# The last half row's queries in two parts, with ScalarE taking all weights in every second step

## The chip, the cores and the metric

The kernel runs on one core of a Trainium2 chip. Its engines work side by side, each through its own list of instructions in order: PE (TensorE: matrix products, with a separate row PEld for its weight loads), DVE (VectorE), ACT (ScalarE), POOL (GpSimd) and SP (SyncE, which here only issues DMAs). The metric is device time in microseconds. An effect on a few operations near the end of one stage is measured against a run of over 1.6 ms, so the numbers below are kept to tenths and hundredths of a microsecond.

## The reference, cut to what matters

The model has two attention and two feed-forward layers on x of shape (4, 1024, 256), all in float32. The change touches the second attention layer and the hand-over to the last layer, a mixture of experts:

```python
def _L1_attn_ref(x, w_qkv, w_out, b_out, gamma, beta):   # 16 heads of 16
    q, k, v = ...                                        # from x @ w_qkv
    scores = einsum('bhqd,bhkd->bhqk', q, k) / sqrt(16)
    w = relu(scores)
    attn = w / (sum(w, axis=-1, keepdims=True) + 1e-6)
    out = einsum('bhqk,bhkd->bhqd', attn, v) ... @ w_out + b_out
    return layernorm(x + out) * gamma + beta

x = x + layernorm(L1_attn(layernorm(x)))
x = x + layernorm(L1_ffn(layernorm(x)))                  # experts

# in L1_ffn, for all 4096 tokens together:
S = sigmoid(xt @ Wg).T          # 8 experts x 4096 tokens
G, I = top_k(S, 1024)           # each expert picks its tokens
```

So every token must have passed the whole attention layer, its layer norms and the gating product before any expert can choose its tokens: the top-k needs all logits.

## The kernel before

**Stages.** The first attention and feed-forward layer fill the span up to about 418 us, the second attention layer (the pool `st3` in the code) runs to about 1096 us, then come a search for each expert's threshold, the gathers, and the experts. Tokens are worked in blocks of 512 (`TB`), two to a sequence (`BPB = 2`); the text calls a block a half row, `t` = 0 to 7. A block has four tiles of 128 tokens (`NJ = 4`).

**A step of the attention.** For each half row the loops run over four groups of heads (`NG = 4`, four heads each) and eight tiles of keys (`KT = 8`): 32 steps. `scores` (L1233) writes four 32-row products of 512 queries into four PSUM banks at once; two of the banks (`sc1`) go through relu on ScalarE (L1242, 128x512 each), the other two (`sc2`, one 128x1024 tile) on VectorE (L1243). `weigh` (L1249) multiplies the weights with the values, four products into the four 32-row bands of the accumulator `po`. Program order on PE is scores of step n+1, then weighing of step n. The profile counts two instructions for each float32 product, so a step's four products appear as x8. The three banks with the tag "s" serve both the single scores (two a step) and, through `side`, all other products of the stage.

**After a group** `finish` turns `po` back (L1281); after every second group `divide` puts two pieces in front of the list `rest`: `by_weight` (L1110 to L1112, the division by the sum) and `back` (L1120, which writes `oT`). After the last group `close` adds the output projection `project_out` (L1135, added to the residual at L1142), and for each of the four tiles: `stats_y` (L1064 to L1067: statistics on VectorE, the power -1/2 on POOL), `affine` (L1155, L1156), a second statistics piece, `shift` (L1160 on VectorE, L1162 on ScalarE), `add` (L1167), `stats_x`, and `token_rows` (L1178, with DMAs to `tok_d` and `x_d`). Then come `turn_gating` (PE transposes, L1193, a ScalarE copy, L1196) and `gate` (L1207, added into `logits` at L1215).

**What sets the order.** PE, VectorE and ScalarE run in the order in which the code is written out (`manual_schedule`). Pieces wait in two lists, `beside` (with PE work) and `rest`. `go_on(room)` takes one piece of `beside`, if there is one, and `room` pieces of `rest`, double after a piece of `beside`; the main loop calls it once a step, with room 1, or 0 in a group's last step. So a half row's closing pieces run beside the steps of the next half row. The last half row has no next one: its pieces run after the last step, with `keep_busy` (L206, idle products of 512 columns in bfloat16) on PE, 8 and 63 of them. DMA issues on SP are placed by the framework.

**Afterwards** the gating stage begins with `keep_busy(idle, 9)` and 15 rounds of a threshold search on VectorE, with one small PE product each.

Of the kernel before, what the change touches and what calls it, by code (L numbers as in the profile page):

```python
# [18 lines left out]
P = 128  # L19
D = 256  # L20
# [51 lines left out]
def kernel(  # L72
# [968 lines left out]
    with ExitStack() as st3:  # L1041
# [25 lines left out]
            nc.gpsimd.tensor_tensor(rs, ve, mhalf[:, 0:1], ALU.pow)  # L1067
            return mv[:, 0:1], rs

        def by_tile(*steps):  # L1070

            kept = {}

            def run(do, i):
                kept[i] = do(i, *kept.get(i, ())) or ()

            return [lambda do=do, i=i: run(do, i) for do in steps for i in range(NJ)]

        def normalize(row, b, k):

# [21 lines left out]

        def divide(state, t):

            got, oT, closing = state["turned"], state["oT"], state.get("close")
            even = wk.tile([P, TB // 32, 2, HD], F32, tag="even", name="even", bufs=1)

            def by_weight():
                den = small.tile([P, 2, TB // 32], F32, tag="den", name="den")
                nc.vector.tensor_scalar(den, got[:, :, :, HD], KEPS, None, ALU.add)  # L1110
                nc.vector.reciprocal(den, den)
                nc.vector.tensor_tensor(  # L1112
                    even.rearrange("p b r d -> p r b d"),
                    got[:, :, :, 0:HD],
                    den.unsqueeze(3).to_broadcast([P, 2, TB // 32, HD]),
                    ALU.mult,
                )

            def back():
                nc.vector.transpose(oT[:, t, :], even.rearrange("p b r d -> p (b r d)"))  # L1120
                if t:
                    beside.extend(closing)

            return [by_weight, back]

        def close(t, h, oT):

            y = wk.tile([P, NJ, D], F32, tag="y", name="y")

            def project_out(z):  # L1130
                pt = side([P, 2, D], "pt")
                for k in range(2):
                    i = 2 * z + k
                    for c in range(DC):
                        nc.tensor.matmul(  # L1135
                            pt[:, k, :],
                            lhsT=oT[:, c, i * P : (i + 1) * P],
                            rhs=wop[:, c, :],
                            start=(c == 0),
                            stop=(c == DC - 1),  # L1140
                        )
                nc.vector.tensor_tensor(y[:, 2 * z : 2 * z + 2, :], pt, h[:, 2 * z : 2 * z + 2, :], ALU.add)  # L1142
                for k in range(2):
                    after(2 * z + k)

            def after(i):
                rest.append(after_out.pop(0))
                if i == NJ - 1:
                    rest.extend(after_out)

            def stats_y(i):
# [20 lines left out]
            def token_rows(i, mean, rs):  # L1172
                if t < ADDED:
                    nc.sync.dma_start(out_flat[t][:, i, :], xs[t][:, i, :])
                if i == 0:
                    gating["h"] = wk.tile([P, NJ, D], F32, tag="hg", name="hg")
                hg = gating["h"][:, i, :]
                nc.vector.tensor_scalar(hg, xs[t][:, i, :], mean, rs, ALU.subtract, ALU.mult)  # L1178
                nc.sync.dma_start(tok_d[t * TB + i * P : t * TB + (i + 1) * P, 0:D], hg)
                if i == NJ - 1:  # L1180
                    nc.sync.dma_start(x_d[t * TB : (t + 1) * TB, :].rearrange("(j p) d -> p j d", p=P), xs[t])
                if i % 2:
                    beside.append(lambda: turn_gating(i - 1))
                if i == NJ - 1:
                    beside.append(gate)

            def turn_gating(i0):
                if i0 == 0:
                    gating["hT"] = wk.tile([P, DC, TB], F32, tag="hT", name="hTg")
                tp = side([P, DC, 2, P], "tpg")  # L1190
                for c in range(DC):
                    for i in range(2):
                        nc.tensor.transpose(  # L1193
                            tp[:, c, i, :], gating["h"][:, i0 + i, c * P : (c + 1) * P], ident
                        )
                nc.scalar.copy(  # L1196
                    gating["hT"][:, :, i0 * P : (i0 + 2) * P], tp.rearrange("p c i t -> p c (i t)")
                )

            def gate():  # L1200

                b, half = divmod(t, BPB)
                pg = side([P, SEG], "pg")
                for c in range(DC):
                    for u in range(TB // SEG):
                        z = half * (TB // SEG) + u
                        nc.tensor.matmul(  # L1207
                            pg[32 * z : 32 * (z + 1), :],
# [2 lines left out]
                            start=(c == 0),  # L1211
                            stop=(c == DC - 1),
                        )
                rows = slice(64 * half, 64 * (half + 1))
                nc.vector.tensor_tensor(logits[rows, :], logits[rows, :], pg[rows, :], ALU.add)  # L1215

            gating = {}
            after_out = by_tile(
                stats_y, affine, lambda i: scale_of("c", y[:, i, :]), shift, add, stats_x, token_rows
            )  # L1220

            for z in range(2):
                yield lambda z=z: project_out(z)

        def scores(row, qh, g, kt):

            t, r = divmod(g, 2)
            w = wts.tile([P, 4, TB], F32, tag="w", name="w")
            singles = [ps.tile([P, TB], F32, tag="s", name="sc1", bufs=3) for _ in range(2)]
            pair = ps.tile([P, 2, TB], F32, tag="d", name="sc2", bufs=2)  # L1230
            for j, sc in enumerate((*singles, pair[:, 0, :], pair[:, 1, :])):
                rows = slice(32 * j, 32 * (j + 1))
                nc.tensor.matmul(  # L1233
                    sc,
                    lhsT=row["kT"][t][rows, r, kt * P : (kt + 1) * P],
                    rhs=row["qT"][rows, t, qh * TB : (qh + 1) * TB],
                    start=True,
                    stop=True,
                )

            for j, sc in enumerate(singles):
                nc.scalar.activation(w[:, j, :], sc, AF.Relu)  # L1242
            nc.vector.tensor_scalar(w[:, 2:4, :], pair, 0.0, None, ALU.max)  # L1243
            return w

        def weigh(row, g, kt, w):
            t, r = divmod(g, 2)
            for j in range(4):
                nc.tensor.matmul(  # L1249
                    po[32 * j : 32 * j + HD + 1, :],  # L1250
                    lhsT=row["v"][:, kt, HQ * t + 2 * j + r, :],
                    rhs=w[:, j, :],
                    start=(kt == 0),
                    stop=(kt == KT - 1),
                )

# [3 lines left out]
        def go_on(room=1):  # L1262
# [3 lines left out]
            for _ in range(room):  # L1266
                if rest:
                    rest.pop(0)()

        state = {}  # L1270

        def finish(row, b, qh, g, kt, w):
            t, r = divmod(g, 2)
            if g == 0 and kt == 0:
                state["oT"] = wk.tile([P, DC, TB], F32, tag="oT", name="oT")
            weigh(row, g, kt, w)
            if kt == KT - 1:

                if r == 0:
                    state["turned"] = wk.tile([P, 2, TB // 32, 32], F32, tag="turned", name="turned")  # L1280
                nc.vector.transpose(state["turned"][:, r].rearrange("p b d -> p (b d)"), po)  # L1281
                if g == NG - 1:
                    state["close"] = [
                        *close(b * BPB + qh, row["h"][qh], state["oT"])
                    ]
                if r:
                    rest[:0] = divide(state, t)

        row = row0
# [3 lines left out]
        for b in range(B):  # L1293
            after = open_row() if b + 1 < B else None
            for qh in range(BPB):
# [2 lines left out]
                    nc.scalar.activation(spare, row["h"][qh][:, 0, 0:1], AF.Exp)  # L1298
                if after is not None:
                    *steps, last = normalize(after, b + 1, qh)  # L1300
                    rest.extend((*steps, lambda last=last, to=(after, qh): (last(), beside.extend(project(*to)))))
                for g in range(NG):
                    for kt in range(KT):
                        w = scores(row, qh, g, kt)
                        if before is not None:
                            finish(*before)

                        go_on(0 if kt == KT - 1 else 1)
                        before = (row, b, qh, g, kt, w)
            row = after  # L1310
        finish(*before)
        idle = ps.tile([P, 2, TB], F32, tag="d", name="idle", bufs=2)[:, 0, :]
        keep_busy(idle, 8)
        while rest and not beside:
            go_on()
        while beside:
            go_on()

        keep_busy(idle, 63)
        while beside or rest:  # L1320
            go_on()
    both.close()


# [2 lines left out]
    with ExitStack() as st4:  # L1327
# [27 lines left out]
        with ExitStack() as sa:  # L1355
# [7 lines left out]
            nc.vector.tensor_scalar(sc, sc, 1.0, None, ALU.add)  # L1363
            nc.vector.reciprocal(sc, sc)
            idle = ps.tile([P, TB], F32, tag="idle", name="idle", bufs=1)
            keep_busy(idle, 9)

            def by_token(src, name):
                pt = ps.tile([P, SEG // P, NSEG * NE], F32, tag="tp", name=name)
# [450 lines left out]
```

## Time and profile before

| what | us |
|---|---|
| median of 3 runs (1630.39 to 1633.67) | 1633.25 |
| the profiled execution | 1633.18 |
| its span, first to last instruction | 1631.2 |
| last half row, first scores (L1233) start | 993.82 |
| its last weighing (L1249) ends | 1069.48 |
| last addition into the logits (L1215) ends | 1096.26 |

Times inside the run are counted from the start of the span. In the lists of instructions each line gives start, length, engine, line of the code, operation, what is written and read with its shape, the count where several like instructions are merged, and in brackets how long the engine had been idle before and what ended that. In the chain of work that ended last, each piece is followed back to what released it; lines give start, length, engine and what was done. Groups give the total busy time and the mean in ns of one.

### The profile page before, as it was taken

To read this page: it belongs to the slowest core of one execution; us is meant where nothing else is said; L and a number is where in the kernel's file an instruction comes from. 1 tells how busy PE (TensorE), PEld (TensorE's weight loads), DVE (VectorE), ACT (ScalarE), POOL (GpSimd) and SP (SyncE) were. 2 spreads that over 40 slices of the span, in tenths; PEclk is the share of its full clock that TensorE was granted. 3 is DMA by queue.
4 is the path that set the end of the run, shared out by engine and by line. 5 is a ranking of instruction groups with operands and counts; after the bars stand their busy time and mean duration, and the time that the engine had idled before them with its cause. 6 is when DMAs were issued, how large, how long until landed. Compare 5 with 4: busy or idle time off the path is not lost.

```text
span 1631.2 us, 22623 instructions
## 1 busy us (share of the span) xinstructions
PE 1569.7 (96%) x8787; PEld 778.2 (48%) x8787; DVE 920.7 (56%) x2085; ACT 634.7 (39%) x1101; POOL 403.3 (25%) x439
## 2 busy tenths in 40 slices
PE   7999999999999999999999999983999999999997
PEld 3666666666322232222323222231757667566674
DVE  4555566664657787878787888878211211222145
ACT  3344444544544545454545454521121121211233
POOL 4123232222201011111111001010423324324555
PEclk9999999999999999999999999995999999999999
DMA  8300000000000000101010100040133233234355
GB/s 205 120 1 1 1 1 1 0 1 1 1 1 1 23 18 7 34 7 34 1 40 1 39 2 27 14 168 4 53 78 69 66 74 72 66 75 89 65 148 136
DMA packets 70069, 71.15 MB, mean 44 GB/s; under 512 B 23597, under 2 KB 62922, under 8 KB 69834
## 3 DMA queue, kind: packets, MB, share of 16 engines
q1 hardware_dynamic: 56080, 47.01, 9.4%
q0 software_dynamic: 13008, 21.77, 7.4%
q8 instruction: 69, 1.13, 0.3%
q10 hardware_dynamic: 874, 0.93, 0.2%
q14 instruction: 38, 0.31, 0.1%
HBM read 41.74 MB, written 27.95 MB: 43 GB/s over the span
## 4 chain that ended last, share of the span: by engine, by line
PE 92%; DVE 4%; issue 1%; POOL 1%; ACT 1%; DMA 1%; POOLq 0%; SPq 0%; DVEq 0%; ACTq 0%
PE sc L1233 16%; PE po L1249 16%; PE ph L1712 13%; PE py L1735 13%; PE pg L691 4%; PE py L799 4%; PE pv L707 3%; PE ph L855 2%; PE po L771 2%; PE pt L1135 2%; PE pv L380 2%; PE pq L356 2%; PE pq L876 2%; PE po L775 2%; PE pk L356 2%; PE pkv L786 1%
## 5 line engine op out<-in xcount | busy, mean ns | idle before, releaser
L1243 DVE TENSOR_SCALAR w<-sc 128x1024 f32<-128x1024 f32 x256 | 312.7, 1222 | 97.4 <-PE sc L1233 65.1
L1242 ACT ACTIVATE w<-sc 128x512 f32<-128x512 f32 x512 | 278.0, 594 | 229.6 <-PE sc L1233 102.5
L1233 PE MATMUL sc<-qT,kT 32*128 32x512 f32 x2048 | 293.6, 639 | 1.4 <-ACT w L1242 0.8
L1249 PE MATMUL po<-w,vaug 128*17 128x512 f32 x2048 | 274.7, 598 | 1.3 <-DVE turned L1281 0.3
L1735 PE MATMUL py<-w,hid 128*128 128x256 f32 x1024 | 230.1, 380 | 0.0
L1719 ACT ACTIVATE hid<-ph,mb 128x512 f32<-128x512 f32 (+1 forms) x136 | 90.1, 662 | 344.4 <-PE ph L1712 343.3
L1712 PE MATMUL ph<-xT,w 128*128 128x512 f32 (+1 forms) x544 | 222.8, 567 | 0.7 <-DVE xT L1696 0.7
L1735 PEld LDWEIGHTS py<-w,hid 128*128 128x128 f32 x1024 | 191.1, 190 | 32.0 <-issue 7.0
L1233 PEld LDWEIGHTS sc<-qT,kT 32*128 32x128 f32 x2048 | 80.7, 183 | 184.9 <-issue 170.7
L1712 PEld LDWEIGHTS ph<-xT,w 128*128 128x128 f32 x544 | 103.2, 190 | 111.1 <-issue 107.6
L1249 PEld LDWEIGHTS po<-w,vaug 128*17 128x17 f32 x2048 | 35.3, 95 | 200.3 <-issue 171.0
L1754 POOL DMA_INDIRECT acc_d<-y,idx x56 | 88.1, 1573 | 157.0 <-issue 131.8
L1752 DVE TENSOR_TENSOR y<-py,mb 128x256 f32<-128x256 f32 x56 | 23.4, 418 | 142.3 <-PE py L1735 140.3
L1521 POOL DMA_INDIRECT got<-tok_d,idx x64 | 65.8, 1028 | 152.1 <-DVE idx L1511 135.0
L1696 DVE COPY xT<-tp 128x512 f32<-128x512 f32 (+1 forms) x34 | 22.3, 660 | 91.7 <-PE tp L1691 91.7
L1067 POOL TENSOR_TENSOR rsg<-veg,mhalf 128x1 f32<-128x1 f32 x32 | 17.7, 554 | 219.5 <-DVE veg L1066 219.5
L691 PE MATMUL pg<-nT,wh 128*128 128x512 f32 x128 | 61.4, 611 | 1.5 <-ACT nT L630 1.5
L799 PE MATMUL py<-wo,oT 128*128 128x256 f32 x256 | 61.9, 385 | 0.0
L707 PE MATMUL pv<-wh,nT 128*128 128x512 f32 x128 | 59.7, 592 | 0.0
L1511 DVE CAST idx<-parts 128x8 int32<-128x8 f32 x8 | 1.3, 167 | 101.8 <-PE parts L1509 101.8
L799 PEld LDWEIGHTS py<-wo,oT 128*128 128x128 f32 x256 | 47.3, 190 | 17.2 <-issue 9.4
L572 POOL TENSOR_TENSOR x<-x,y 128x1024 f32<-128x1024 f32 x14 | 32.9, 2351 | 73.3 <-ACT y L561 73.3
(277 smaller groups left out, 1927.5 us busy)
## 6 DMA issues: line engine op xcount, KB each, us to landing
w<-in_L_ffn_W_dram SPq DMA_DIRECT2D x16, 1024.0 KB, 5.7
x<-in_L_attn_x_dram SPq DMA_DIRECT2D x8, 512.0 KB, 5.0
acc_d<-logits SPq DMA_DIRECT2D x8, 512.0 KB, 4.2
x_d<-x SPq DMA_DIRECT2D x8, 512.0 KB, 3.0
tok_d<-hg SPq DMA_DIRECT2D x32, 128.0 KB, 1.7
back_w<-acc_d SPq DMA_DIRECT2D x6, 512.0 KB, 7.4
out_dram<-x SPq DMA_DIRECT2D x20, 128.0 KB, 1.7
out_dram<-back_w POOLq DMA_DIRECT2D x4, 512.0 KB
```

Source lines behind the costliest of these rows:

```text
L691: nc.tensor.matmul(pg, lhsT=wh[:, c, HID + e * P : HID + (e + 1) * P], rhs=d["nT"][:, c, :], start=(c == 0), stop=(c == DC - 1),)
L707: nc.tensor.matmul(pv, lhsT=d["nT"][:, c, i * P : (i + 1) * P], rhs=wh[:, c, 0:HID], start=(c == 0), stop=(c == DC - 1),)
L799: nc.tensor.matmul(py, lhsT=d["oT"][:, e, :], rhs=wo[:, e, :], start=(e == 0), stop=(e == EC - 1))
L1233: nc.tensor.matmul(sc, lhsT=row["kT"][t][rows, r, kt * P : (kt + 1) * P], rhs=row["qT"][rows, t, qh * TB : (qh + 1) * TB], start=True, sto ...
L1242: nc.scalar.activation(w[:, j, :], sc, AF.Relu)
L1243: nc.vector.tensor_scalar(w[:, 2:4, :], pair, 0.0, None, ALU.max)
L1249: nc.tensor.matmul(po[32 * j : 32 * j + HD + 1, :], lhsT=row["v"][:, kt, HQ * t + 2 * j + r, :], rhs=w[:, j, :], start=(kt == 0), stop=(kt ...
L1521: return nc.gpsimd.indirect_dma_start(out=dst, out_offset=None, in_=rows[:, :], in_offset=self.at_chunk(c), bounds_check=NT - 1, oob_is_er ...
L1712: nc.tensor.matmul(ph, lhsT=w1[:, c, f * P : (f + 1) * P], rhs=xT[u][:, c, h * n : (h + 1) * n], start=(c == 0), stop=(c == DC - 1),)
L1719: nc.scalar.activation(hid[:, f, h * n : (h + 1) * n], ph, AF.Gelu, bias=mb1[:, e * FC + f : e * FC + f + 1])
L1735: nc.tensor.matmul(py, lhsT=hid[:, f, i * P : (i + 1) * P], rhs=w2[:, f, :], start=(f == 0), stop=(f == FC - 1),)
L1754: scatter = nc.gpsimd.indirect_dma_start(out=acc_d[:, :], out_offset=lists[e].at_chunk(k), in_=y, in_offset=None, bounds_check=NT - 1, oob ...
```

## The change

Only the last half row (`b = 3`, `qh = 1`) is worked otherwise (`halves = 2`); all others keep their order.

- Its 512 queries are taken in two parts of 256 (`q2`). A step takes two tiles of keys at once, so that a scores bank still holds 512 columns: two key tiles by 256 queries. There are 16 such double steps in each part, 32 together. `weigh` writes one half of `po`'s columns, the left for even groups, the right for odd ones.
- In every second of these steps ScalarE computes all weights (two 128x512 and one 128x1024 instruction) and VectorE none.
- Pieces beside these steps are dealt by time: each piece carries an estimate `us` of VectorE's time, and `go_on_for` takes pieces until the step's allowance is used up: 0.9 us in a step whose weights are shared, 1.8 (1.5 at a group's end) in one where ScalarE has them all; up to 0.3 is carried on.
- The closing pieces of the first part (tiles 0 and 1) run beside the steps of the second. The second part (tiles 2 and 3) closes in `at_once`: projection by halves of the contraction, `keep_busy` 4 and 34, the layer norms of two tiles interleaved, the shift on VectorE in place of ScalarE, statistics of two tiles with one power on POOL.
- `x_d` for this half row is stored in two DMAs.
- The gating stage starts with `keep_busy(idle, 13)` in place of 9.

```diff
+        VECTOR_US = {"affine": 0.9, "shift": 0.43, "add": 0.42, "token_rows_and_on": 0.35}
...
+                go.us = VECTOR_US.get(do.__name__, 0.65)
...
         def divide(state, t):
...
+            by_weight.us, back.us = (0.7, 0.45) if n < TB else (1.3, 0.75)
...
+                if i == tiles[-1]:
+                    js = slice(tiles[0], tiles[-1] + 1)
+                    rows = x_d[t * TB : (t + 1) * TB, :].rearrange("(j p) d -> p j d", p=P)
+                    nc.sync.dma_start(rows[:, js, :], xs[t][:, js, :])
...
+            def moments(tag, src, part):
...
+                if part == "take":
+                    for k, i in enumerate(tiles):
+                        nc.vector.bn_stats(st[:, k, :], src[:, i, :])
+                    for k in range(2):
+                        nc.vector.bn_aggr(mv[:, k, :], st[:, k, :])
+                    nc.vector.tensor_scalar(ve[:, :, 0], mv[:, :, 1], EPS, None, ALU.add)
+                    nc.gpsimd.tensor_tensor(rs[:, :, 0], ve[:, :, 0], mhalf[:, 0:2], ALU.pow)
+                return [(i, mv[:, k, 0:1], rs[:, k, :]) for k, i in enumerate(tiles)]
+
+            def at_once(by_weight, back):
+                x, stt = xs[t], nc.vector.scalar_tensor_tensor
+                pts = [(i, side([P, D], "pt")) for i in tiles]
+                for i, pt in pts:
+                    project_tile(pt, i, (0,))
+                idle = ps.tile([P, 2, TB], F32, tag="d", name="idle", bufs=2)[:, 0, :]
+                keep_busy(idle, 4)
+                by_weight()
+                back()
+                for i, pt in pts:
+                    project_tile(pt, i, (1,))
+                keep_busy(idle, 34)
+                for i, pt in pts:
+                    nc.vector.tensor_tensor(y[:, i, :], pt, h[:, i, :], ALU.add)
+                scales = moments("b", y, "take")
+                for i, mean, rs in scales:
+                    stt(y[:, i, :], y[:, i, :], mean, gam, ALU.subtract, ALU.mult)
+                for i, mean, rs in scales:
+                    stt(y[:, i, :], y[:, i, :], rs, bet, ALU.mult, ALU.add)
+                scales = moments("c", y, "take")
+                for i, mean, rs in scales:
+                    nc.vector.tensor_scalar(y[:, i, :], y[:, i, :], mean, None, ALU.subtract)
+                for i, mean, rs in scales:
+                    stt(x[:, i, :], y[:, i, :], rs, x[:, i, :], ALU.mult, ALU.add)
+                for i, mean, rs in moments("g", x, "take"):
+                    token_rows(i, mean, rs)
+                turn_gating(tiles[0])
+                gate()
...
+        def scores(row, qh, q2, halves, g, kt):
...
+            for m in range(halves):
+                for j, sc in enumerate((*singles, pair[:, 0, :], pair[:, 1, :])):
+                    rows = slice(32 * j, 32 * (j + 1))
+                    nc.tensor.matmul(
+                        sc[:, m * n : (m + 1) * n],
+                        lhsT=row["kT"][t][rows, r, (kt + m) * P : (kt + m + 1) * P],
+                        rhs=row["qT"][rows, t, q0 : q0 + n],
...
+            if halves > 1 and kt // halves % 2:
+
+                nc.scalar.activation(w[:, 2:4, :], pair, AF.Relu)
+            else:
+                nc.vector.tensor_scalar(w[:, 2:4, :], pair, 0.0, None, ALU.max)
...
+        def go_on_for(us, weights_on_act):
+
+            left = min(spare_time[0], 0.3) + us
+            if beside:
+                beside.pop(0)()
+                left -= 0.45
+            while rest:
+
+                takes = 0.8 if weights_on_act and rest[0].us == VECTOR_US["shift"] else rest[0].us
+                if takes > left:
+                    break
+                left -= takes
+                rest.pop(0)()
+            spare_time[0] = left
...
+                halves = 2 if (b, qh) == (B - 1, BPB - 1) else 1
+                for q2 in range(halves):
+                    for g in range(NG):
+                        for kt in range(0, KT, halves):
+                            w = scores(row, qh, q2, halves, g, kt)
+                            if before is not None:
+                                finish(*before)
+
+                            at_end = kt == KT - halves
+                            if halves == 1:
+                                go_on(0 if at_end else 1)
+                            elif kt // halves % 2:
+                                go_on_for(1.5 if at_end else 1.8, True)
+                            else:
+                                go_on_for(0.9, False)
+                            before = (row, b, qh, q2, halves, g, kt, w)
             row = after
         finish(*before)
-        idle = ps.tile([P, 2, TB], F32, tag="d", name="idle", bufs=2)[:, 0, :]
-        keep_busy(idle, 8)
-        while rest and not beside:
-            go_on()
-        while beside:
-            go_on()
-
-        keep_busy(idle, 63)
         while beside or rest:
             go_on()
+        state["close"][0](*divide(state, DC - 1))
...
-            keep_busy(idle, 9)
+            keep_busy(idle, 13)
```

## The prediction

> **What bounds the kernel now.** I read first the page's head, for the size of the thing:
>
> ```profile
> span 1631.2 us, 22623 instructions
> PE 1569.7 (96%) x8787; PEld 778.2 (48%) x8787; DVE 920.7 (56%) x2085; ACT 634.7 (39%) x1101; POOL 403.3 (25%) x439
> ```
>
> PE is nearly always busy, but that says little here: part of that busy time is the idle matmuls of `keep_busy`. So I went to the chain that ended last, in order of time, from 1062 to 1097 us (start, length, what):
>
> ```profile
> 1063.81 1.07 PE sc L1233 x8
> 1064.88 0.98 PE po L1249 x8
> ...
> 1068.50 1.03 PE po L1249 x8
> 1069.53 0.02 issue
> 1069.55 0.73 DVE turned L1281
> ...
> 1072.40 3.30 PE pt L1135 x14
> ...
> 1075.73 0.69 DVE y L1142
> ...
> 1095.84 0.44 DVE logits L1215
> ```
>
> Two regimes meet at 1069.5. Before it, a step is scores then weighing, 1.07 + 0.98 = 2.05 us, both PE. After it, PE has nothing but `pt`, four-tile transposes and idle matmuls; VectorE's layer norms of the last half row carry the chain to the last `logits` at 1096.26. Call E the end of the last `po` (1069.48): the **tail** is 1096.26 - 1069.48 = 26.8 us. Everything later (threshold rounds, gathers, experts) starts from `logits`, so the change moves the end by what it does to E plus what it does to the tail. The last half row's first scores start at 993.82 (timeline).
>
> Third, the timeline inside one steady step:
>
> ```profile
> 1062.89 1.08 ACT L1242 ACTIVATE w<-sc 128x512 f32<-128x512 f32 x2 [0.97 <-ACT w L1242]
> 1063.01 1.22 DVE L1243 TENSOR_SCALAR w<-sc 128x1024 f32<-128x1024 f32 x1
> 1063.73 1.14 PE L1233 MATMUL sc<-qT,kT 32*128 32x512 f32 x8
> ```
>
> ScalarE starts its weights 1.21 us after the scores start and is free half of the step; VectorE has 0.83 us beside its 1.22.
>
> **Part 1, the tail.** It now holds two tiles, not four, and none of the previous half row's work. Dealing out the pieces by the new budgets step by step, the previous half row's last piece (`gate`) falls in the seventh step of the second part and the first part's last piece, its `gate`, in the very last step; nothing is left over. Tail from E, with durations from this trace (128x512 operations 0.69 to 0.71, 128x256 0.40 to 0.48, of which 0.33 to 0.40 is the distance to an independent next one): `turned`, `den`, reciprocal, `even`, `oT` at half width 0.44+0.18+0.26+0.43+0.43 and 0.16 of gaps, 1.9; second halves of the two projections until both `y` are added, 1.6; three rounds of statistics, each 0.37+0.37+0.18+0.20+0.13, 3.75; four affine operations 1.65; two subtractions and two additions 1.6; the last power, which VectorE awaits (0.55 on POOL and two hops), 0.8; two `hg` 0.8; transposes 0.6; ScalarE copy 0.7; gating 0.9; `logits` 0.6. Sum **14.9**, say 15.0: 11.8 less than before. The first two powers hide behind the operations that need only the mean. The 4 and 34 idle matmuls (34 x 0.22 = 7.5) end some 2 us before the transposes need PE, so they hide; so does the growth from 9 to 13 afterwards: at the 0.23 each of 1096.3 to 1098.4 they end 3.0 after `logits`, and the transposes of `sc` come at 3.4. Without the full clock (13 of them took 5.33 us at 1130) they would be late by about 2 us.
>
> **Part 2, E moves later.** The same 32 steps run (16 double ones twice), each with 16 matmul instructions of 256 columns in each slot in place of 8 of 512. Work formerly in the tail now stands between steps on PE. Side work before: `tpg` 2 x 0.59, `pg` 0.96, `pt` 2 x 1.93 = 6.0. After: `tpg` 4 x 0.59, `pg` 0.96+0.96+0.48, `pt` 3 x 1.93 = 10.55. Before: 993.82 + 32 x 2.05 + the first `po` 1.05 + 6.0 + 3.0 of waits = 1069.5, as measured. The waits after, worked out by placing each dealt piece on its engine: 0.8 at the table load, as now; in an odd step ScalarE needs two weights at 0.50 and a 128x1024 one, done 1.21 + 2.03 = 3.24 after the scores begin, where `po` wants it at 2.05 + 1.07 = 3.12, so with the hop 0.17 in the six odd steps without other cover, 1.0; five places where a shift or `hTg` copy also stands in ScalarE's queue, 1.95; four where pieces stand before an even step's VectorE weights, 1.2; and the last step, odd and with no scores after it to cover ScalarE, 0.75. Sum 5.7. The `turned` waits go, since groups alternate between column halves of `po`. E = 993.82 + 65.6 + 1.05 + 10.55 + 5.7 = 1076.7; the same laying-out of the old order comes out 0.4 early, so **1077.1**, 7.6 later.
>
> The 128x1024 relu on ScalarE is not in the trace. Nearest rows:
>
> ```profile
> L1243 DVE TENSOR_SCALAR w<-sc 128x1024 f32<-128x1024 f32 x256 | 312.7, 1222 | 97.4 <-PE sc L1233 65.1 <-ACT x L1162 15.5 <-issue 12.5
> L1242 ACT ACTIVATE w<-sc 128x512 f32<-128x512 f32 x512 | 278.0, 594 | 229.6 <-PE sc L1233 102.5 <-ACT w L1242 96.2 <-issue 26.5
> L1719 ACT ACTIVATE hid<-ph,mb 128x512 f32<-128x512 f32 x120 | 82.5, 687 | 329.6 <-PE ph L1712 329.3
> L1719 ACT ACTIVATE hid<-ph,mb 128x256 f32<-128x256 f32 x16 | 7.6, 474 | 14.8 <-PE ph L1712 14.0 <-issue 0.8
> ```
>
> The last two give 213 ns for 256 columns: 594 + 426 = 1.02. Bounds: 0.9 to 1.2, which is 0.5 us less to 1.5 more over the half row. The Trainium skill ("ScalarE: Activation LUTs", rules for kernel authors) speaks against this edit: relu belongs on VectorE. Here the rows say otherwise, 1222 ns there against 1.02 here, for float32 out of PSUM; by the rule each odd step would lose, by the rows VectorE gains 1.22 for pieces.
>
> **The half-width matmuls** are the disputed term: twice the weight loads for the same columns. The skill ("TensorE: Matmul & The Clock Gate", Part 3) has weight loads overlap running matmuls only in another row group, and its load price, columns over 1.2, is 107 ns for 128 columns and 14 for 17. Two more loads per tile and slot, uncovered, are then 0.21 + 0.03 = 0.24 per step, 32 x 0.24 = 7.7 us (an estimate from that page); by the trace's 183 and 95 ns a load, 0.56 and 18 us. But the timeline shows runs of tiled 256-column matmuls:
>
> ```profile
> 339.28 1.13 PE L855 MATMUL ph<-pT,v 64*128 64x256 f32 x8
> ...
> 347.43 3.67 PE L876 MATMUL pq<-hid,u 128*64 128x256 f32 x32
> 351.04 1.13 PE L786 MATMUL pkv<-v,packed 128*128 128x512 f32 x2
> ```
>
> A full-array 256-column instruction takes 0.216 (L799, eight in 1.73). L855, two row tiles with four in sequence each, lasts 1.06 to its successor: 0.86 and 0.20. L876, two column tiles with sixteen each, lasts 3.61: 3.46 and 0.15. So the excess belongs to the slot, not to each of its loads, and a slot of four in sequence costs 1.07, as `sc` does with two. I take 0 by these rows, with 0 to 0.24 kept for the range; four tiles at once with 16 loads is not shown.
>
> **Other moves.** Everything before the last half row has its order unchanged. On SP's queue the last `x_d` store becomes two of 256 KB, the first some 20 us earlier; behind the second waits the last expert load, issued at 1089.51, while no expert product runs before 1148.6, so it hides. ScalarE's shifts become VectorE subtractions in the tail only.
>
> **Sum.** -11.8 + 7.6 = -4.2 us. `logits` end near 1092.1, the span 1627.0; with the 2.0 around it (1633.18 for the profiled execution) 1629.0, and that execution lies on the median of 1633.25. 0.2% is 3.3 us, about what a measurement can tell from no change.
>
> **Rivals.**
> - *Weight loads come uncovered* (slower). Place: the second half of each `sc` and `po` slot; price 0.24 a step; 1629.0 + 7.7 = 1636.7. It decides from 4.2 / 32 = 0.13 a step. For it: the rule, and 183 ns per load row against 213 per matmul. Against: L855 and L876. Chance 0.10.
> - *ScalarE or VectorE bunch worse.* The 4.2 of waits on ScalarE and VectorE double, since true piece costs pass the budgets (statistics 0.75 against 0.65, affine 0.98 against 0.9): 1633, no change. For it: the 1.2 us lost once already to such a bunch at 1016. Against: VectorE's whole load in the half row is 16 x 1.22 and some 40 of pieces, 60 of 83 us. Chance 0.15.
> - *The waits dissolve* because one late step gives the next slack: 3 less, 1626. Chance 0.15.
> - *Pieces left over*, so the tail isn't halved: the tally excludes it unless the queues differ from what I read; inside the first chance.
>
> Likeliest, as summed: 0.60, own range 1627 to 1631.5. Faster by over 0.2%: 0.47 of it, all of the third, 0.02 of the second: 0.64. Within: 0.13 + 0.12 = 0.25. Slower: 0.10 + 0.01 = 0.11. Range 1625 to 1634: it holds the third case's middle and the second's, and leaves out the first.
>
> **What will show it.** `sc` and `po` slots of 1.07 and 0.98 with 16 instructions (1.2 and up: the loads show); a 128x1024 ScalarE row near 1.02; first scores to E 83 us; E to `logits` 15; idle matmuls at 0.21 to 0.23. It is wrong if even steps without side work exceed 2.2, if PE's waits on ScalarE sum to over 6, or if transposes in the tail run at half clock (each such run about 1 us).

## The result, and the profile after

The changed kernel takes **1625.18 us** (median of 5 runs, 1624.72 to 1626.83); the kernel before takes 1631.44 us (5 runs, 1630.39 to 1633.67, the three of the table above among them). The ratio is 0.9959, 95% interval 0.9945 to 0.9974: faster by 0.41%, or by 4.2 to 9.0 us. The forecast was 1629.0 us and a gain of 4.2 us; the measured gain of 6.3 us is half as large again, and the time lies at the low end of the range that was given, 1625 to 1634.

The page's head of the changed kernel, first line the span, second the busy times:

```profile
span 1623.5 us, 23583 instructions
PE 1562.3 (96%) x9270; PEld 797.6 (49%) x9270; DVE 904.9 (56%) x2080; ACT 647.6 (40%) x1115; POOL 402.0 (25%) x436
```

There are 483 more PE instructions (512 from the halving in the last half row, less 29 idle ones), yet PE is busy 7.4 us less; its share is 96% as before and still tells nothing. The chain of work that ended last does. Of the changed kernel, 1061 to 1090 us (start, length, engine and work):

```profile
1061.61 1.08 PE sc L1303 x16
1062.69 0.99 PE po L1329 x16
...
1070.89 1.17 PE sc L1303 x16
1072.06 1.07 ACT w L1312 x2
1073.12 0.93 ACT w L1315
...
1074.09 1.07 PE po L1329 x12
...
1075.19 0.46 DVE turned L1379
...
1077.12 0.71 PE pt L1145 x2
...
1077.86 0.42 DVE y L1264
...
1089.53 0.44 DVE logits L1233
```

Three things are to be seen. The steps take 1.08 and 0.99 us with 16 instructions, where they took 1.07 and 0.98 with 8. The last step (from 1070.9) is carried by ScalarE, since it alone makes the weights there. And from the last `po` to the last `logits` the chain is now short. In numbers, with the same marks as before the change (E is the end of the last `po`):

| us, from each kernel's profiled execution | before | after | difference | forecast |
|---|---|---|---|---|
| first scores of the last half row start | 993.82 | 993.55 | -0.27 | 0 |
| steps, from there to E | 75.66 | 81.58 | +5.92 | +7.6 |
| tail, E to the last `logits` | 26.78 | 14.83 | -11.95 | -11.8 |
| last `logits` to the first expert product (`ph`) | 52.37 | 51.80 | -0.57 | 0 |
| last PE product to the span's end | 11.41 | 10.59 | -0.82 | 0 |

The stretch between the last two rows, the experts, is 471.2 in both. What the change does by its order of work is 5.92 - 11.95 = **-6.03 us**. The first, fourth and fifth row, another -1.7 us, are differences between two single executions: the start lies between 993.1 and 994.6 in the ten profiled executions of this study, all of the same work up to there; the fifth row is 10.5 to 10.6 in every profile but the one of before; and the fourth depends on when TensorE's clock comes back, which is taken up below. The medians, 6.3 us apart, lie nearer to the -6.03 than to the 7.7 by which the two profiled spans differ; the interval of the ratio holds both.

The groups of the weights, by form, over all eight half rows (total busy us, mean ns of one, then the idle time ahead of them):

```profile
L1317 DVE TENSOR_SCALAR w<-sc 128x1024 f32<-128x1024 f32 x240 | 293.2, 1222 | 99.2 <-PE sc L1303 71.1 <-ACT x L1173 13.4 <-issue 10.7
...
L1315 ACT ACTIVATE w<-sc 128x1024 f32<-128x1024 f32 x16 | 16.5, 1029 | 0.0
```

VectorE has 240 relus where it had 256, ScalarE 16 new ones of 1029 ns; these 16 are those of the last half row.

### The profile page after: what moved, and what is told of

It reads as the page before. It is cut to its first block, busy times and chain, and to the rows that moved or that the text cites. A ratio compares the mean times of both kernels' runs of the same rounds, so it can differ in the third digit from the quotient of the medians.

```text
span 1623.5 us, 23583 instructions
## 1 busy us (share of the span) xinstructions
PE 1562.3 (96%) x9270; PEld 797.6 (49%) x9270; DVE 904.9 (56%) x2080; ACT 647.6 (40%) x1115; POOL 402.0 (25%) x436
## 4 chain that ended last, share of the span: by engine, by line
PE 92%; DVE 3%; issue 2%; POOL 1%; ACT 1%; DMA 0%; POOLq 0%; SPq 0%; ACTq 0%; DVEq 0%
PE sc L1303 17%; PE po L1329 16%; PE ph L1819 13%; PE py L1842 13%; PE py L799 4%; PE pg L691 4%; PE pv L707 3%; PE ph L855 2%; PE po L771 2%; PE pt L1145 2%; PE pv L380 2%; PE pq L356 2%; PE pq L876 2%; PE po L775 2%; PE pk L356 2%
## 5 line engine op out<-in xcount | busy, mean ns | idle before, releaser
L1317 DVE TENSOR_SCALAR w<-sc 128x1024 f32<-128x1024 f32 x240 | 293.2, 1222 | 99.2 <-PE sc L1303 71.1
L1303 PE MATMUL sc<-qT,kT 32*128 32x512 f32 (+1 forms) x2304 | 294.7, 586 | 1.5 <-ACT w L1312 0.8
L1329 PE MATMUL po<-w,vaug 128*17 128x512 f32 (+1 forms) x2304 | 276.1, 550 | 1.0 <-ACT w L1315 0.3
L1303 PEld LDWEIGHTS sc<-qT,kT 32*128 32x128 f32 x2304 | 94.4, 183 | 173.9 <-issue 157.9
L1329 PEld LDWEIGHTS po<-w,vaug 128*17 128x17 f32 x2304 | 44.8, 95 | 191.5 <-issue 157.5
```

The source lines that it names most:

```text
L1303: nc.tensor.matmul(sc[:, m * n : (m + 1) * n], lhsT=row["kT"][t][rows, r, (kt + m) * P : (kt + m + 1) * P], rhs=row["qT"][rows, t, q0 : q0 ...
L1329: nc.tensor.matmul(po[32 * j : 32 * j + HD + 1, weighed(halves, r)], lhsT=row["v"][:, kt + m, HQ * t + 2 * j + r, :], rhs=w[:, j, m * n : ...
```

## The experiments

Each kernel below is the changed kernel with the edit shown. The times are medians, and the ratios are to the kernel before, timed on the same chip: 1631.4 us (5 runs) for the change, 1632.4 (42 runs) for the next four kernels, 1632.8 (9 runs) for the last four. Since the change was not timed again on the other two chips, the ratios are the fairer comparison with it. "Steps" and "tail" are the marks of the table, from one profiled execution each.

| kernel | time, us | ratio to before, 95% interval | steps | tail |
|---|---|---|---|---|
| the change | 1625.2 | 0.9959, 0.9945 to 0.9974 | 81.58 | 14.83 |
| e_relu_dve | 1630.1 | 0.9984, 0.9978 to 0.9991 | 85.44 | 15.06 |
| e_count | 1629.5 | 0.9985, 0.9978 to 0.9992 | 87.14 | 15.69 |
| e_pieces | 1628.6 | 0.9974, 0.9964 to 0.9984 | 81.58 | 17.20 |
| e_both | 1625.7 | 0.9958, 0.9942 to 0.9975 | 80.30 | 15.69 |
| e_nowarm | 1626.8 | 0.9966, 0.9952 to 0.9980 | 81.58 | 16.05 |
| e_warm | 1626.7 | 0.9962, 0.9947 to 0.9976 | 81.59 | 14.83 |
| e_best | 1625.0 | 0.9954, 0.9937 to 0.9970 | 80.30 | 14.83 |
| e_rounds | 1623.3 | 0.9940, 0.9923 to 0.9957 | 80.31 | 14.83 |

### e_relu_dve: VectorE keeps its half of the weights in every step

```diff
-            if halves > 1 and kt // halves % 2:
+            if False:
                 nc.scalar.activation(w[:, 2:4, :], pair, AF.Relu)
```

> The changed kernel with every step's 128x1024 weights on VectorE; the dealing of pieces stays. Theory (VectorE's time is what the odd steps buy): VectorE then has 16 x 1.22 = 19.5 us more to do in the half row, 79 of 82 us, so PE waits for it; first scores to the end of the last weighing grows from 81.6 to about 85.3, tail unchanged at 14.8, time about 1629. Rival (the pieces fit beside shared steps anyway, and ScalarE's odd steps cost PE 1.5 us of waits): 80 us, time 1624.

Steps 85.44 us, tail 15.06, time 1630.1. The part with ScalarE taking all weights is worth 85.44 - 81.58 = 3.9 us: without it more than half of the change's gain is gone. The allowances of the odd steps (1.8 and 1.5 us of VectorE's time) were left as they are, so a part of the 3.9 may be pieces dealt to steps that no longer have room for them; no run deals them anew. What PE waited for in the last half row's steps, summed by the instruction that released it (total us, times, longest):

```profile
PE po L1329 <- DVE turned L1379: 2.0, 4, 0.8
PE po L1329 <- DVE w L1317: 0.7, 2, 0.4
```

The first line refutes a sentence of the prediction, which let the `turned` waits go because groups alternate between column halves of `po`. They don't go: the first `po` of a group still waits for VectorE's transpose of the group before. In the changed kernel the same list has no such wait: VectorE, with 16 relus fewer, comes to that transpose in time.

### e_count: pieces dealt by number, as before, in place of by time

```diff
-                                go_on_for(1.5 if at_end else 1.8, True)
+                                go_on(2)
...
-                                go_on_for(0.9, False)
+                                go_on(1)
```

> The changed kernel with pieces dealt by count (one in an even step, two in an odd one, double after a piece with PE work) in place of VectorE's estimated time; nothing is left over at the end. Theory: PE waits oftener for bunches of pieces, about 3 us more: 84.6 from first scores to the last weighing, tail 14.8, time 1628. Rival (order of pieces is indifferent while VectorE is idle a quarter of the time): 81.6, time 1625.

Steps 87.14 us in the profiled execution, 2.5 more than expected. The timeline of this execution shows two causes (start, length, what, and in brackets the idle time before it):

```profile
1010.60 1.22 DVE L1317 TENSOR_SCALAR w<-sc 128x1024 f32<-128x1024 f32 x1
...
1011.73 0.44 DVE L1379 STREAM_TRANSPOSE turned<-po 128x256 f32<-128x256 f32 x1
...
1012.23 1.88 PE L1329 MATMUL po<-w,vaug 128*17 128x256 f32 x16 [1.75 <-DVE turned L1379]
```

This relu is for scores that PE began at 1006.69; ScalarE started its share of them at 1007.90. On VectorE it stood behind an addition, three statistics pieces and an affine piece, busy from 1006.79 to 1010.60 without a break. So the relu is 2.7 us late, the transpose behind it too, and PE waits 1.75 us. Then the same 16 instructions that take 1.06 elsewhere take 1.88: the granted clock is 0.55 in the stretch from 1012 to 1015. This slot is 0.68 too long by the clock, and the `pg` slot after it 0.90 (1.86 for 0.96). The profiled execution (1632.8 us) is one of 4 out of 18 that lie between 1632.7 and 1632.9; the other 14 lie between 1628.7 and 1630.6. The granted clock is 0.984 to 0.986 in those four and 0.988 in each of the fourteen. So I take 1.6 off the steps, 85.5, for an execution that keeps its clock, 0.9 above the expected 84.6; this is argued from the two groups, since no execution of the fourteen was profiled. Dealing by time is then worth 85.5 - 81.58 = 3.9 us, and the two ratios, 0.26% apart, say 4.2. Another wait of 1.4 us, for a relu of VectorE, lies in the same steps.

### e_pieces: the second part closes in pieces, as before, not in `at_once`

```diff
-                at_end = state["at_end"] = q2 == 1
+                at_end = state["at_end"] = False
...
+        idle = ps.tile([P, 2, TB], F32, tag="d", name="idle", bufs=2)[:, 0, :]
+        keep_busy(idle, 8)
+        while rest and not beside:
+            go_on()
+        while beside:
+            go_on()
+        keep_busy(idle, 40)
         while beside or rest:
             go_on()
-        state["close"][0](*divide(state, DC - 1))
```

> The changed kernel whose second part closes tile by tile as in the kernel before (idle matmuls 8 and 40), not both tiles at once. Theory: most of the 12 us off the tail come from halving it, and some 3 from interleaving two tiles with one power in place of two: tail 18, time 1628.5. Rival (the interleaving does it): tail over 20, time over 1630; or (halving alone does it) tail 15, time 1625.

Tail 17.20, steps unchanged to 0.01 us. So of the tail's 11.95, 26.78 - 17.20 = 9.6 come from halving what is left after the last step, and 2.4 from closing with `at_once`. Some 0.5 of the 2.4 is clock and not the interleaving: the last `pg` takes 1.53 us here in place of 1.05, with a granted clock of 0.57 in the three microseconds from its start. The time, 1628.6, is 3.5 above that of the changed kernel; by the ratios, 0.15%, it is 2.4.

### e_both: two of the waits on ScalarE taken away

In the last odd step VectorE gets its relu back, and the shift of this half row goes to VectorE (its pieces dealt by 0.43 us each) so that it doesn't stand in ScalarE's queue.

```diff
+                if t >= NB - 2:
+                    nc.vector.tensor_scalar(y[:, i, :], y[:, i, :], mean, None, ALU.subtract)
+                    return (rs,)
...
-            if halves > 1 and kt // halves % 2:
+            if halves > 1 and kt // halves % 2 and (q2, g, kt) != (1, NG - 1, KT - halves):
...
-                takes = 0.8 if weights_on_act and rest[0].us == VECTOR_US["shift"] else rest[0].us
+                takes = rest[0].us
```

> The changed kernel with two repairs of ScalarE's waits: the very last step shares its weights with VectorE, and the closing pieces beside the last half row's steps subtract the mean on VectorE in place of ScalarE's shift. Theory (waits for ScalarE are about half of PE's 4.4 us of waits there): first scores to last weighing 79.1 in place of 81.6, tail 14.8, time 1622.7. Rival (VectorE's longer pieces bunch instead): 81 to 82, time 1625.

Steps 80.30: 1.28 less, where 2.5 were expected. What a shift costs is to be seen in the timeline of the changed kernel:

```profile
1028.53 0.51 ACT L1173 ACTIVATE x<-x,msc 128x256 f32<-128x256 f32 x1 [1.43 <-DVE msc L1171]
...
1028.94 1.06 ACT L1312 ACTIVATE w<-sc 128x512 f32<-128x512 f32 x2
1028.97 1.74 PE L1303 MATMUL sc<-qT,kT 32*128 32x256 f32 x16
...
1030.64 1.38 PE L1329 MATMUL po<-w,vaug 128*17 128x256 f32 x16
1030.80 0.91 ACT L1173 ACTIVATE x<-x,msc 128x256 f32<-128x256 f32 x2
...
1031.60 1.09 ACT L1312 ACTIVATE w<-sc 128x512 f32<-128x512 f32 x2
...
1031.95 1.44 PE L1303 MATMUL sc<-qT,kT 32*128 32x256 f32 x16
```

The shift at 1028.53 puts off the next weights, and the scores at 1028.97 and the weighing at 1030.64 become 0.60 and 0.33 us longer than the usual 1.07 and 0.98; the two shifts at 1030.80 put off the weights after those, and the scores at 1031.95 become 0.30 longer. With one more such slot behind two shifts at 1062.16, shifts cost 1.55 us in the half row.

In e_both all of this is gone, and 0.34 of what VectorE's pieces cost. But where the shifts' waits stood, the smaller wait of an odd step, in which ScalarE has all weights, now shows: 0.97 us at eight steps, where the changed kernel has 0.59 at five. And the last step gained nothing. From its scores to E it takes 3.66 us in place of 4.31, but in the changed kernel the first part's gating product `pg` runs inside that step, while ScalarE makes the weights; here the pieces were dealt faster, and `pg` stands ahead of the last scores (in this kernel `pg` is L1227, `sc` L1306, `po` L1332):

```profile
1069.55 1.03 PE L1227 MATMUL pg<-hTg,wgp 128*32 128x256 f32 x4
1070.50 1.15 PE L1306 MATMUL sc<-qT,kT 32*128 32x256 f32 x16
...
1071.58 2.58 PE L1332 MATMUL po<-w,vaug 128*17 128x256 f32 x32
```

With its 0.95 us the same work takes 4.61, 0.3 more. Together this is -1.55 - 0.34 + 0.38 + 0.30 = -1.2 of the 1.28.

And the tail grew to 15.69 where nothing in it was edited. In this kernel `tpg` is L1212, `pg` L1227:

```profile
1086.02 0.78 PE L1212 MATMUL tpg<-ident,hg 128*128 128x128 f32 x4 [1.39 <-DVE hg L1192]
1087.47 1.92 PE L1227 MATMUL pg<-hTg,wgp 128*32 128x256 f32 x4 [0.68 <-ACT hTg L1215]
1089.90 5.03 PE L206 MATMUL idle<-same_b 128*128 128x512 bf16 x13 [0.52 <-DVE logits L1236]
```

The same three lines of the changed kernel:

```profile
1086.90 0.87 PE L1209 MATMUL tpg<-ident,hg 128*128 128x128 f32 x4 [1.30 <-DVE hg L1189]
1088.44 1.05 PE L1224 MATMUL pg<-hTg,wgp 128*32 128x256 f32 x4 [0.67 <-ACT hTg L1212]
1090.01 2.96 PE L206 MATMUL idle<-same_b 128*128 128x512 bf16 x13 [0.52 <-DVE logits L1233]
```

PE pauses after the idle products for 1.39 us in one and 1.30 in the other. In the first the four `pg` products then take 1.92 us in place of 1.05, and the 13 idle ones 5.03 in place of 2.96: half clock. Stretches of 3 us of the two kernels (after the times: busy time of PE, PEld, DVE, ACT and POOL, the granted clock, the DMA share and GB/s), first the experiment, then the changed kernel:

```profile
1087.00:1090.00 3.00, 2.01 (x5) 0.74 (x6) 0.43 (x1) 0.42 (x1) 0.00 (x0) 0.55 0.68 178
1090.00:1093.00 3.00, 3.00 (x8) 1.04 (x8) 2.39 (x4) 0.42 (x1) 0.00 (x0) 0.50 1.01 333
```

```profile
1087.00:1090.00 3.00, 1.82 (x8) 0.80 (x9) 0.59 (x2) 0.59 (x1) 0.00 (x0) 1.00 0.77 204
1090.00:1093.00 3.00, 2.96 (x13) 1.17 (x12) 2.28 (x4) 0.42 (x1) 0.00 (x0) 1.00 0.85 271
```

0.55 and 0.50 against 1.00. The slower `pg` alone makes 0.86, the whole growth of this tail. So the kernel that saves 1.28 us in its steps gives most of it back in this execution, and its time is that of the changed kernel. Of its four runs, the one with a granted clock of 0.988 took 1623.6 us, the three with 0.986 took 1625.5 to 1628.3.

### e_nowarm and e_warm: less and more idle work in the tail

e_nowarm takes the idle products in `at_once` away:

```diff
-                keep_busy(idle, 4)
...
-                keep_busy(idle, 34)
```

> The changed kernel without the 4 and 34 idle matmuls of the tail. Theory (PE's pause then lasts over 9 us and its clock drops to half before the closing transposes and the gating product): first scores to last weighing 81.6 as before, tail 15.9 to 16.5 in place of 14.8, the 13 idle matmuls after it at about 0.43 each instead of 0.23, so that they end 2 us after the transposes of the gates want PE; time 1628. Rival (idle matmuls make no difference this late): 1625.

The timeline of e_nowarm at the end of the tail:

```profile
1087.29 1.22 PE L1209 MATMUL tpg<-ident,hg 128*128 128x128 f32 x4 [8.65 <-DVE hg L1189]
1089.19 1.92 PE L1224 MATMUL pg<-hTg,wgp 128*32 128x256 f32 x4 [0.68 <-ACT hTg L1212]
1091.62 4.21 PE L206 MATMUL idle<-same_b 128*128 128x512 bf16 x13 [0.52 <-DVE logits L1233]
```

Both `tpg` (1.22 for 0.87) and `pg` (1.92 for 1.05) run at half clock (granted 0.50 from 1084 to 1093), and the tail is 16.05, as expected. The idle products in the tail are thus worth 1.2 us there. The time is 1626.8, not the 1628 expected: the 13 idle products took 4.21 us and not the 5.6 that I had counted.

e_warm lengthens the run of idle products so that the pause ahead of `tpg` vanishes:

```diff
-                keep_busy(idle, 34)
+                keep_busy(idle, 40)
```

> The changed kernel with 40 idle matmuls in the tail in place of 34, which ends them just before the transposes want PE. Theory (a pause of 1.3 us before the transposes is where the clock drops in some executions and not in others): tail 14.8 in every look, the gating product at 1.05, time 1624.5 or a little under the changed kernel's, with less scatter. Rival (34 are enough; the difference between looks comes from elsewhere): 1625.2, same scatter.

The pause is gone and the tail is 14.83. The time isn't lower than that of the changed kernel (1626.7; the ratios are 0.03% apart, well inside their intervals). Its runs lie within 0.8 us, those of the changed kernel within 2.1, which five runs each can't tell apart. This run shows that six more idle products do no harm in the tail, and not that they gain.

### e_best: e_both and the 40 idle products

```diff
         (the edit of e_both)
...
-                keep_busy(idle, 34)
+                keep_busy(idle, 40)
```

> Both repairs of ScalarE's waits (last step shared, mean subtracted on VectorE) with 40 idle matmuls in the tail. Theory: first scores to last weighing 80.3, tail 14.8, time 1623.3; about 1.5 us under the changed kernel. Rival (the gain of the repairs is chance): 81.6 and 1625.

80.30 + 14.83 = 95.13 from the first scores to `logits`, 1.28 less than the change, as the parts say. In time this is 1625.0 with a ratio of 0.9954, which can't be told from the change's 0.9959.

### e_rounds: PE kept busy through the threshold search too

After the last `logits` the 15 rounds of the search use PE for one small product each, and at their end 13 idle products and then two transposes (`placeT`) follow. e_best, with six idle products after each round's product:

```diff
                 nc.tensor.matmul(pn, lhsT=same_b, rhs=n, ...)
+                keep_busy(idle, 6)
```

> The same as the kernel before it in this list, with six idle matmuls behind the small product of each round of the threshold search, so that PE's clock is not at half when the search ends. Theory: the 13 idle matmuls after the search take 2.8 us in place of 4.7 to 5.3, the transposes of the places come up to 1.6 us sooner; from the last logits to the first expert product 50.8 us in place of 51.8 to 53.0, time 1621.8. Rival (they delay the small products of the rounds by queueing ahead of them): each of 15 rounds longer than 1.98 us, time over 1625.

1623.3 us, ratio 0.9940: 1.7 us below e_best, and each of its four runs is below each of e_best's four. It has the lowest ratio of the study, though its interval still overlaps that of the change. The search's end in the changed kernel:

```profile
1124.01 4.68 PE L206 MATMUL idle<-same_b 128*128 128x512 bf16 x13
...
1127.13 0.42 DVE L1553 TENSOR_TENSOR upto<-upto,mask 128x256 f32<-128x256 f32 x1
...
1128.52 0.38 PE L1478 MATMUL placeT<-ident,upto 128*128 128x128 f32 x2
```

and in e_rounds:

```profile
1123.21 2.97 PE L206 MATMUL idle<-same_b 128*128 128x512 bf16 x13
...
1126.33 0.42 DVE L1557 TENSOR_TENSOR upto<-upto,mask 128x256 f32<-128x256 f32 x1
1126.81 0.44 PE L1481 MATMUL placeT<-ident,upto 128*128 128x128 f32 x2 [0.64 <-DVE upto L1557]
```

In the changed kernel `upto` is there at 1127.55, and the transposes start 0.97 later, behind idle products that should have filled a gap and at half clock (granted 0.50 from 1124 to 1127) overfill it. In e_best, on which the edit was laid, it is 1.66. In e_rounds they start 0.06 after it and wait for `upto`, not for PE. From `logits` to the first expert product it takes 50.86 us, against 51.5 to 53.0 in the profiles of the other nine kernels. The profiles' mean granted clock is 0.997 there, 0.984 to 0.988 in the others.

## Why the prediction was right or wrong

**The step that failed is the sum of PE's waits in "Part 2, E moves later":** 5.7 us placed one by one, and 0.4 carried over from laying out the old order. The mechanism was right, the size was not: the 81.58 us of steps leave 81.58 - 65.6 - 1.05 - 10.55 = 4.38 for these waits, 1.7 less than 6.1. Place by place, as time of a slot above its usual length:

| place | forecast | measured |
|---|---|---|
| table load | 0.8 | 0.69 |
| ScalarE alone with all weights | 1.0, six places | 0.59, five places (0.13 to 0.14 at four, 0.06 at one) |
| a shift or copy in ScalarE's queue | 1.95, five places | 1.55, four slots, all behind shifts |
| pieces before VectorE's weights | 1.2, four places | 0.74, three places (0.31, 0.34 and 0.09) |
| last step | 0.75 | 0.73: 0.26 of waiting, and `pg` 0.47 longer than priced |
| carried over from the old order | 0.4 | 0.1, all that is left |

One place where ScalarE alone makes the weights, with nothing else in its way:

```profile
1055.10 1.15 PE L1303 MATMUL sc<-qT,kT 32*128 32x256 f32 x16
...
1056.18 1.18 PE L1329 MATMUL po<-w,vaug 128*17 128x256 f32 x16
...
1057.29 1.15 PE L1303 MATMUL sc<-qT,kT 32*128 32x256 f32 x16
```

The weighing holds PE for 1.11 us, 0.13 over its 0.98, where 0.17 was priced. Fewer places cost time than were counted, and most of these cost less. That a late step gives the next one's weights more time, the rival "the waits dissolve" (1626), is seen at one place: right behind a late weighing, the one at 1025.87 waits 0.06 in place of 0.13. How much of the 1.7 is such slack and how much is delays that were priced too high, the runs don't separate. I had given this rival 0.15; it is the one nearest to what happened.

The row of the last step agrees by luck. The first part's `pg` was priced at 0.48 us, half of the 0.96 of a whole half row's, but it takes 0.95 (e_both shows it alone). It fills time in which PE would have waited for ScalarE, so the wait is as much smaller as `pg` is longer.

**The base was off as well.** I laid the forecast's -4.2 on the profiled execution's 1633.2, while the median over more runs is 1631.4 to 1632.8. The miss of 3.8 us in time is so made up of about 1.7 of base (against the 1631.44), 1.7 of waits and 0.2 of tail; the gain, which is a difference, was missed by the last two alone. The median that I had compared it with was one of three runs, and those reached from 1630.4 to 1633.7. In the 42 runs of the kernel before, the time goes with the granted clock: the 13 at 0.988 have a median of 1631.3, the 14 at 0.986 one of 1633.5. The profiled execution was at 0.986, that of the changed kernel at 0.988.

**The tail** held: 14.83 against 15.0, a fall of 11.95 against 11.8. "Nothing is left over" held too, since no work of another part stands behind E.

**The half-width matmuls**, the disputed term, cost next to nothing: slots that nothing disturbs average 1.075 and 0.989 us, against 1.071 and 0.983 before, 0.01 a step and some 0.3 in all. The rule of the Trainium skill ("TensorE: Matmul & The Clock Gate", Part 3), taken as the prediction took it, gave 0.24 us a step, 7.7 in all; the rows of L855 and L876 gave 0. The timeline of the changed kernel, a `po`, the next scores and the next `po` without side work between them:

```profile
1017.42 1.06 PE L1329 MATMUL po<-w,vaug 128*17 128x256 f32 x16
...
1018.41 1.15 PE L1303 MATMUL sc<-qT,kT 32*128 32x256 f32 x16
...
1019.48 0.41 PE L1329 MATMUL po<-w,vaug 128*17 128x256 f32 x4
```

From start to start the slots take 0.99 and 1.07 us, as with 8 instructions of 512 columns. The measurement decides, against the rule as it was taken; the same section also lets loads into a background buffer go ahead, and whether that is what happens here no run shows. The slower rival falls with it.

**The 1024-column relu on ScalarE** was put at 1.02 us and measures 1.03, against 1.22 on VectorE. The rule of the Trainium skill that speaks against this edit ("ScalarE: Activation LUTs", rules for kernel authors; it names bf16 as its case) doesn't hold for these float32 values: e_relu_dve, with relu back on VectorE, loses 3.9 us.

**"ScalarE or VectorE bunch worse"** (1633) didn't happen in the changed kernel, but e_relu_dve and e_count each bring a part of it about (1630.1 and 1629.5): it is kept away by the ScalarE weights and by dealing by time together. The sentence that let the `turned` waits go was wrong, as shown above, and cost nothing only for the same reason.

**Idle matmuls.** The prediction noted that without the full clock the 13 idle ones would be late by about 2 us, and took the clock for granted. In the changed kernel's profile it held; in e_both's and e_count's it didn't.

## What to carry to other kernels

When delays at many places on one engine are added up, lay the steps out one behind the other and ask at each place whether the engine would still be waiting; here the plain sum was 40% too high. The same holds for a repair: when the waits behind the shifts were taken away, smaller ones that they had covered came out. Lay a forecast on the median of several runs, and use a profiled execution only for differences. Where a stage leaves TensorE idle for microseconds ahead of work that the end waits for, look at the granted clock in stretches of a few microseconds: six idle products a round bought 1.7 us here, more than any repair of the steps.

## What the runs showed of the hardware

**The clock after a short pause.** Pauses of nearly the same length have both outcomes: 1.30 us ahead of `tpg` left the full clock in the changed kernel's profile (`pg` 1.05), 1.31 cost part of it in e_relu_dve's (1.28), 1.39 and 1.40 halved it in those of e_both and e_count (1.92 and 1.91), and in e_pieces 1.20 and another 0.28 were followed by `pg` at 1.53. In the steps of e_count a wait of 1.75 was followed at once by half clock. The Trainium skill ("TensorE: Matmul & The Clock Gate", Part 1) has the clock fall after an idle window of about 3.4 us that runs freely; windows that run freely would fit pauses of one length ending in both ways, but here the clock fell when PE was idle for 1.39 and 0.68 us with 0.78 of work between, and never for 3.4 at a stretch. Whether the difference lies in the pause's length or in where the window stood, these runs don't show.

**What stays open.** Why the first scores of the last half row start anywhere between 993.1 and 994.6 us wasn't looked into. That, and the clock at the search's end, make up most of the differences between two executions of one kernel, and changes under about 2 us, such as those of e_warm and e_best, are inside them.
